# A three-stage attention block: first key products ahead of the queries, feature sums on GpSimd, and a new order around them

## The chip, the core and the metric

The kernel runs on one core of a Trainium2 chip. A core has a matrix engine (TensorE, in profiles PE, with its weight loads as PEld), a vector engine (DVE), a scalar engine (ACT), GpSimd (POOL) and a queue engine (SP) that here only starts transfers. PE writes to PSUM, eight banks of 2 KB per partition; DVE and ACT read PSUM, POOL doesn't. The metric is the device time of one execution in microseconds, lower is better.

## The reference

One token array x (512 x 512, float32) goes through three residual layers.

```python
x = x + _L0_xattn_ref(_layernorm(x), ctx, ctx, ...)   # 16 heads of 32, 8192 context rows, softmax
x = x + _L0_attn_ref(_layernorm(x), ...)              # linear attention
x = x + _L0_ffn_ref(_layernorm(x), ...)               # 512 -> 2048 -> 512, quantized, gelu
...
q_proj = _elu1(jnp.einsum('bhnd,hdf->bhnf', q, proj_matrix))   # 128 features for each head
k_proj = _elu1(jnp.einsum('bhnd,hdf->bhnf', k, proj_matrix))
kv = jnp.einsum('bhnf,bhnd->bhfd', k_proj, v)
attn = jnp.einsum('bhnf,bhfd->bhnd', q_proj, kv)
k_sum = k_proj.sum(axis=2)
z = 1.0 / (jnp.einsum('bhnf,bhf->bhn', q_proj, k_sum) + 1e-08)
```

The quantized layer needs the smallest and largest value of its whole input before it can scale it, and of its whole hidden layer before the second product.

## The kernel before, in words

P = 128 partitions; the 512 tokens are four tiles t (NT), the 512 columns four groups c or g (NE) of four heads each (HG). The context is read in 16 blocks of 512 rows. Every PE, DVE, ACT and POOL instruction wrapped in `in_order` stays in the order in which the program text issues it on its engine; each engine then waits only for data and free buffers.

**Opening.** `load_w` (L130), `load_cols` and `load_ctx` (L309) put the transfers on SP's queue: x, Wq, bq, Wk, context block 0, bk, Wv, block 1 and the small rows. DVE normalizes x (`norm_factors`, L150 on: mean and variance, square root on ACT, reciprocal, one correction step). PE transposes it (L349), DVE and ACT copy the result to `xnT`, PE projects the queries (L136) and ACT adds their bias.

**Blockwise products.** Keys and values of a block are made by `blockwise` (L456): a 2 x 2 block scheme with seven products n = 1 to 7, where four need sums of weights (`sums_of_weights`, L373) and of the context (`sums_of_ctx`, L391), both made by POOL. Products 1 and 2 take plain blocks. A product is four steps of four matmuls each (`by_columns`, L403); `evict` then copies or adds its PSUM tile into the four quadrants C11 to C22 of kT or vt, on ACT for the first, on DVE (L493, L496) for the others. Tiles come from `ps_m`, which has two banks. The order is 1, 6, 7, 5, 4, 2, 3.

**Maxima.** Before the loop, `common_maxima` (L583) finds one bound per group g from the scores of 128 keys (L598): two reductions on DVE for each group (L603), then a reduction over groups, a transposition (L614), a second reduction, a diagonal, and a product with ones that spreads it over the partitions (L621). Products of the first values block stand between these: `spread` puts four steps behind each of four groups, `ahead(4)` twice takes four from the queue.

**The loop.** 256 units (block, group, key tile): scores by PE (L757, 64-wide halves), exp by ACT (L766), sums of the weights by DVE (L775), weighted values by PE one unit later (L702). Between scores and weighted values PE takes steps of the next block's products from a queue, as many as `due` says, so that a block is ready when its units start. The last block has its own branch.

**Hand-over.** Output sums of the four token tiles (L867, PSUM tiles `po4`), addition to x and statistics (`added`), normalization in halves of two tiles (`normed`), transposition in halves (`turned_tokens`, L890), then the second attention's values (`values`, L903).

**Linear attention.** For each group g: keys and queries (`projected`, L971), features (`key_features` L1014, `query_features` L1025: PE into the four banks of `ps_f`, ACT exp and relu L993, DVE min and sum L997), `products` (L1038: values times features, and ones times features for the sum over tokens), `turned`, `attended` (L1061), `divided` (a reciprocal L1071). The calls are written out by hand from L1082 on, so that PE makes the next group's keys or queries while ACT and DVE make features. Then the output sums (`out_sums`) and `out_added` with the running extremes.

**Quantized layer.** `norm_factors`, `extremes` (a transposition L1159, a product with ones L1166), rounding and clipping (L1189 to L1194), first product with gelu, extremes again, second product. `keep_busy(n)` issues n bf16 matmuls whose result nobody reads.

A second copy of the program, with exact maxima, follows in an `If` and isn't executed here.

Of the kernel before, what the change touches and what calls it, by code (L numbers as in the profile page):

```python
# [26 lines left out]
def network(  # L27
# [125 lines left out]
    def norm_factors(name, st):  # L153

        n = st.shape[1]

        def op(what, do, *args):
            d = small.tile([P, n], F32, name=f"{name}_{what}", bufs=1)
            in_order(do(d, *args))
            return d  # L160

        mv = small.tile([P, n, 2], F32, name=f"{name}_mv", bufs=1)
        for t in range(n):
            in_order(nc.vector.bn_aggr(mv[:, t, :], st[:, t, :]))
        ve = op("ve", nc.vector.tensor_scalar, mv[:, :, 1], LN_EPS, None, ALU.add)
        sd = op("sd", nc.scalar.activation, ve, AF.Sqrt)
        r0 = op("r0", nc.vector.reciprocal, sd)

        e0 = op("e0", nc.vector.tensor_tensor, r0, r0, ALU.mult)
        e1 = op("e1", nc.vector.tensor_tensor, e0, ve, ALU.mult)  # L170
        e2 = op("e2", nc.vector.tensor_scalar, e1, -0.5, 1.5, ALU.mult, ALU.add)
        rstd = op("rstd", nc.vector.tensor_tensor, r0, e2, ALU.mult)
        return mv[:, :, 0], rstd
# [104 lines left out]
    with ExitStack() as actx:  # L278
# [25 lines left out]

        def load_ctx(b):
            if b >= total:
                return
            ct[b] = ap2.tile([P, NE, KB], F32, name="ct")
            nc.sync.dma_start(  # L309
                ct[b], ctxT[:, ts(b % NB, KB)].rearrange("(c p) k -> p c k", p=P)  # L310
            )
# [4 lines left out]
        wq_sb, wv_sb, wk_sb = place_w(), place_w(), place_w()  # L316
        load_w(Wq, wq_sb)
        bq_sb = load_cols(bq, NE, "bq_sb")
        load_w(Wk, wk_sb)
        load_ctx(0)  # L320
        bk_sb = load_cols(bk, NE, "bk_sb")
# [23 lines left out]
        with tc.tile_pool(name="ps_q", bufs=NE, space=PSUM) as ps_q:  # L345
            pts = [ps_q.tile([P, S], F32, name="pxt") for _ in range(NE)]
            for t in range(NT):
                for c in range(NE):
                    in_order(nc.tensor.transpose(  # L349
                        pts[c][:, ts(t, P)], xn[:, t, ts(c, P)], ident  # L350
                    ))
            for c in range(NE):
                if c % 2 == 0:
                    nc.vector.tensor_copy(xnT[:, c, :], pts[c])
                else:
                    nc.scalar.copy(xnT[:, c, :], pts[c])
        for g in range(NE):
            pq = ps_m.tile([P, S], F32, name="pq", tag="pt")
            project(pq, lambda c: wq_sb[:, c, ts(g, P)], lambda c: xnT[:, c, :])
            nc.scalar.activation(  # L360
                qT[:, g, :], pq, AF.Identity, bias=bq_sb[:, g : g + 1]
            )
# [29 lines left out]

        if not exact:
            of_keys = sums_of_weights(wk_sb)
            sums_of_ctx(0)
            of_values = sums_of_weights(wv_sb)
        for t in range(NT):
            in_order(nc.gpsimd.tensor_add(xs[:, t, :], xs[:, t, :], bo_bc))
# [57 lines left out]
        def blockwise(b, keys):  # L456
# [44 lines left out]
            def evict(n):  # L501
# [3 lines left out]
                if n == 1:  # L505
                    in_order(nc.scalar.copy(C11, ps))
                elif n == 6:
                    add(C12, C11, ps)
# [10 lines left out]
                elif n == 2:  # L519
                    add(C11, C11, ps, 0)  # L520
                elif n == 3:
                    add(C12, C12, ps)
# [10 lines left out]
            for n in (1, 6, 7, 5, 4, 2, 3):  # L533
# [12 lines left out]
            return steps  # L546

# [35 lines left out]
        def common_maxima(mp, ps_x):  # L583
# [22 lines left out]


            steps = blockwise(0, False)
            spread([(g,) for g in range(NE)], scores, steps[: 4 * NE])
            queue[:0] = [(1, step) for step in steps[4 * NE :]]  # L610
            ahead(4)
            in_order(nc.vector.tensor_reduce(top, tops, AX.X, ALU.max))
            pt = ps_x.tile([P, 2, S], F32, name="pm", tag="scm")
            in_order(nc.tensor.transpose(pt[:NE, 0, :P], top, ident))  # L614
            ahead(4)
# [3 lines left out]
            ))  # L619
            pb = ps_x.tile([P, 2, S], F32, name="pb", tag="scm")  # L620
# [59 lines left out]
        with ExitStack() as mctx:  # L680
            mp = mctx.enter_context(tc.tile_pool(name="mp", bufs=1, side="right"))
            ps_x = mctx.enter_context(tc.tile_pool(name="ps_x", bufs=3, space=PSUM))
            for step in keys_of(0) if exact else blockwise(0, True):
                step()
# [215 lines left out]
        def values(t, copy):  # L900
            ps = ps_m.tile([P, E], F32, name="pv2", tag="pt")
            for c in range(NE):
                in_order(nc.tensor.matmul(  # L903
# [14 lines left out]
        for t in range(2, 4):  # L918
            output_sums(po4[t], t, range(NE), Z, wo_sb)
            added(t, po4[t], x_st[1], t - 2)  # L920
        turned_tokens(0)
        normed(1)
        warm_up(AF.Exp)
        values(0, nc.scalar.copy)
        turned_tokens(1)
        values(1, nc.scalar.copy)
# [24 lines left out]
    with ExitStack() as lctx:  # L951
# [14 lines left out]
        kT2, qT2, kf, qf, kvT, kvl = {}, {}, {}, {}, {}, {}  # L966
# [41 lines left out]
        def key_features(g, between):  # L1008

            ps = ps_f.tile([P, HG, S], F32, name="feat")  # L1010
            for t in range(NT):
                for j in range(HG):
                    rows = ts(j, D)
                    in_order(nc.tensor.matmul(  # L1014
                        ps[:, j, ts(t, F)], lhsT=kT2[g][rows, ts(t, P)],
                        rhs=proj_sb[rows, g, :], start=True, stop=True,
                    ))
            kf[g] = elu1(ps, by_head, between)

        def query_features(g, between):  # L1020

            ps = ps_f.tile([P, HG, S], F32, name="feat")
            for j in range(HG):
                rows = ts(j, D)
                in_order(nc.tensor.matmul(  # L1025
                    ps[:, j, :], lhsT=proj_sb[rows, g, :], rhs=qT2[g][rows, :],
                    start=True, stop=True,
                ))
            qf[g] = elu1(ps, by_token, between)

        def products(g):
# [3 lines left out]
            for i in range(2):  # L1035
                for t in range(NT):
                    for j in range(HG):
                        in_order(nc.tensor.matmul(  # L1038
                            ps[ts(j, D), i, :],
                            lhsT=ones_c if i else va[:, t, ds(g * P + j * D, D)],  # L1040
                            rhs=kf[g][:, j, ts(t, F)],
                            start=(t == 0), stop=(t == NT - 1),
                        ))
# [57 lines left out]
        products(3)  # L1101
        att = attended(2, every, (ps_a, "av"))
# [4 lines left out]


        po = [ps_m.tile([P, E], F32, name="po", tag="pt") for _ in range(2)]
# [3 lines left out]

        def out_sums(t, groups):
            output_sums(po[t], t, groups, aT, wout_sb)

        def out_added(t):
# [7 lines left out]
            smallest(x_lo[:, one], xs[:, t, :])  # L1125

        out_sums(0, [0, 1]), out_sums(1, [0, 1])
# [3 lines left out]
        out_sums(2, [0, 1])  # L1131
# [5 lines left out]
        out_sums(3, [0, 1]), out_sums(2, [2, 3]), out_sums(3, [2, 3])  # L1137
# [57 lines left out]


    mean, rstd = norm_factors("y", y_st)
# [17 lines left out]
    mm = extremes("q1", y_ext, (lambda: norm(0), lambda: (norm(1), norm(2))))  # L1215
# [57 lines left out]
    def keep_busy(n):  # L1273


        for _ in range(n):
            in_order(nc.tensor.matmul(
                pys[NT - 1], lhsT=w2_q[:, 0, :P], rhs=w2_q[:, 0, :], start=True, stop=True
            ))

    keep_busy(8)
# [3 lines left out]
    mm = extremes("q2", h_ext, (lambda: keep_busy(1), lambda: keep_busy(6)))  # L1285
# [105 lines left out]
```

## Time and profile before

| | us |
|---|---|
| median of 3 runs (1124.95 to 1125.51) | 1125.46 |
| the profiled execution | 1124.31 |
| its span | 1122.4 |
| opening and queries, to the first key product | 26.9 |
| key products of block 0 | 12.4 |
| maxima | 18.4 |
| the loop to the first output sum | 903.8 |
| hand-over, to the second attention's keys | 24.6 |
| linear attention to the last output sum | 78 |
| quantized layer | 58 |

PE is busy for 1080.2 of the 1122.4 us, DVE for 927.7, ACT for 633.5, POOL for 163.4. A group of the profile is a source line on an engine; `a<-b,c` names the tile written and those read. A float32 matmul of the program shows as two hardware matmuls. The idle time in brackets is that of the engine just before the row, with what ended it.

### The profile page before, as it was taken

How to read it: one execution, taken by the hardware profiler on the slowest of the kernel's cores; microseconds unless marked ns; L12 is line 12 of the kernel's file. 1: busy time of each engine (PE TensorE's matmuls, PEld its weight loads, DVE VectorE, ACT ScalarE, POOL GpSimd, SP SyncE). 2: the span in 40 equal slices, each digit the busy share in tenths (PEclk: the TensorE clock that was granted, in tenths of full speed). 3: DMA queues.
4: the chain of work that ended last, by engine and by line, in shares of the span. 5: the costliest groups of instructions: out<-in, count | busy, mean ns of one | idle time of the engine just before them, and what ended most of it. 6: DMA issues, size and time to landing. Idle time of an engine off the chain costs nothing.

```text
span 1122.4 us, 30765 instructions
## 1 busy us (share of the span) xinstructions
PE 1080.2 (96%) x14207; PEld 407.2 (36%) x14210; DVE 927.7 (83%) x863; ACT 633.5 (56%) x425; POOL 163.4 (15%) x82
## 2 busy tenths in 40 slices
PE   6999999999999999999999999999999999999876
PEld 3433333333333333333333333333332322344332
DVE  3678999998888888888888888888887878656896
ACT  2055555556666666666665555555555566336353
POOL 3430303003303030303030303030300000000000
PEclk9999999999999999999999999999999999999988
DMA  7021222120212030212010101010110021130001
GB/s 262 3 95 58 77 58 96 39 76 30 80 46 68 31 95 30 67 58 67 31 58 2 39 2 40 2 39 2 40 39 2 2 76 39 38 151 1 1 1 40
DMA packets 24744, 55.54 MB, mean 49 GB/s; under 512 B 1952, under 2 KB 2464, under 8 KB 24352
## 3 DMA queue, kind: packets, MB, share of 16 engines
q1 hardware_dynamic: 24320, 52.97, 14.3%
q8 instruction: 113, 1.85, 0.6%
q10 hardware_dynamic: 288, 0.52, 0.1%
q14 instruction: 23, 0.19, 0.1%
HBM read 48.25 MB, written 5.24 MB: 48 GB/s over the span
## 4 chain that ended last, share of the span: by engine, by line
PE 89%; DVE 4%; ACT 4%; issue 1%; DMA 0%; ACTq 0%; DVEq 0%
PE pm L403 36%; PE sc L757 24%; PE av L702 18%; ACT ex L766 4%; PE po L867 2%; PE pq L971 2%; PE pv L903 1%; PE pq L136 1%; DVE unchanged L143 1%; PE pys L1292 1%; DVE de L1071 1%; PE att L1061 1%; PE dn L720 0%; DVE f L997 0%; PE feat L1014 0%
## 5 line engine op out<-in xcount | busy, mean ns | idle before, releaser
L766 ACT ACTIVATE ex<-sc,bias 128x2048 f32<-128x2048 f32 x256 | 504.0, 1969 | 360.8 <-PE sc L757 359.0
L775 DVE TENSOR_TENSOR acc<-acc,ex 128x2048 f32<-128x2048 f32 x248 | 581.6, 2345 | 73.5 <-ACT ex L766 72.8
L757 PE MATMUL sc<-qT,kT 32*64 32x512 f32 x4096 | 285.2, 613 | 6.9 <-ACT ex L766 6.7
L702 PE MATMUL av<-ex,vt 128*32 128x512 f32 x2048 | 266.9, 593 | 0.0
L757 PEld LDWEIGHTS sc<-qT,kT 32*64 32x64 f32 x4096 | 59.7, 129 | 221.8 <-ACT ex L766 199.7
L391 POOL TENSOR_TENSOR tt<-ct 128x512 f32<-128x512 f32 x32 | 55.6, 1738 | 577.7 <-DMA ct<-in_ctxT 399.7
L403 PE MATMUL pm<-w,tt 128*32 128x256 f32 x2048 | 126.8, 382 | 0.0
L403 PE MATMUL pm<-tt,w 128*32 128x256 f32 x1920 | 118.0, 382 | 0.0
L493 DVE TENSOR_TENSOR vt<-vt,pm 128x512 f32<-128x512 f32 x112 | 75.4, 685 | 31.3 <-PE pm L403 30.1
L403 PE MATMUL pm<-w,ct 128*32 128x256 f32 x1536 | 98.7, 383 | 0.0
L391 POOL TENSOR_TENSOR tt<-ct,tt 128x512 f32<-128x512 f32 x32 | 93.3, 2915 | 1.3
L403 PE MATMUL pm<-ct,w 128*32 128x256 f32 x1440 | 92.3, 383 | 0.0
L403 PEld LDWEIGHTS pm<-w,tt 128*32 128x32 f32 x2048 | 59.8, 109 | 86.0 <-issue 53.4
L702 PEld LDWEIGHTS av<-ex,vt 128*32 128x32 f32 x2048 | 65.4, 110 | 55.4 <-issue 14.0
L403 PEld LDWEIGHTS pm<-tt,w 128*32 128x32 f32 x1920 | 56.7, 109 | 77.0 <-issue 45.4
L403 PEld LDWEIGHTS pm<-w,ct 128*32 128x32 f32 x1536 | 43.5, 109 | 72.5 <-issue 48.6
L403 PEld LDWEIGHTS pm<-ct,w 128*32 128x32 f32 x1440 | 41.1, 109 | 67.9 <-issue 44.5
L493 DVE TENSOR_TENSOR kT<-kT,pm 128x512 f32<-128x512 f32 x60 | 40.9, 681 | 27.4 <-PE pm L403 26.4
L496 DVE SCALAR_TENSOR_TENSOR kT<-pm,bk_sb,kT 128x256 f32<-128x256 f32 x90 | 39.1, 474 | 4.5 <-PE pm L403 4.5
L714 DVE TENSOR_TENSOR Z<-Z,av 128x512 f32<-128x512 f32 x60 | 40.7, 678 | 0.0
L993 ACT ACTIVATE er<-feat 128x1024 f32<-128x1024 f32 x32 | 30.2, 1030 | 8.9 <-PE feat L1014 6.7
L997 DVE SCALAR_TENSOR_TENSOR f<-er 128x1024 f32<-128x1024 f32 x16 | 19.4, 1219 | 15.1 <-ACT er L993 15.1
(176 smaller groups left out, 558.0 us busy)
## 6 DMA issues: line engine op xcount, KB each, us to landing
ct<-in_ctxT SPq DMA_DIRECT2D x16, 1024.0 KB, 5.3
wraw<-in_W1T SPq DMA_DIRECT2D x16, 512.0 KB, 3.8
wraw<-in_W2T SPq DMA_DIRECT2D x16, 512.0 KB, 3.7
wd<-wquant SPq DMA_DIRECT2D x16, 256.0 KB, 2.4
w_q<-wd SPq DMA_DIRECT2D x2, 2048.0 KB, 10.5
w<-in_w_qkv SPq DMA_DIRECT2D x3, 1024.0 KB, 5.1
w<-in_Wq SPq DMA_DIRECT2D x1, 1024.0 KB, 7.4
w<-in_Wk SPq DMA_DIRECT2D x1, 1024.0 KB, 9.6
```

The lines of the kernel that those rows point to most:

```text
L391: in_order(nc.gpsimd.tensor_tensor(tt[b][:, i], x, y, ALU.subtract))
L403: in_order(nc.tensor.matmul(ps[ts(j, D)], lhsT=lhsT[:, ts(j, D)], rhs=rhs, start=start, stop=stop))
L493: in_order(nc.vector.tensor_tensor(dst, src, ps, ALU.add))
L496: in_order(nc.vector.scalar_tensor_tensor(dst[:, m, :], ps[:, m, :], bk_sb[:, 2 * i + m : 2 * i + m + 1], src[:, m, :], ALU.add, ALU.add,))
L702: in_order(nc.tensor.matmul(av[g][ts(j, D), :], lhsT=vt[b][:, k, ds(g * P + j * D, D)], rhs=ex[:, j, :], start=(k == 0), stop=(k == NC - 1),))
L714: in_order(nc.vector.tensor_tensor(Z[:, g, :], Z[:, g, :], ps, ALU.add))
L757: in_order(nc.tensor.matmul(sc[ts(h, P // 2), j, :], lhsT=kT[b][rows, g, ds(k * P + h * P // 2, P // 2)], rhs=qT[rows, g, :], start=not ex ...
L766: in_order(nc.scalar.activation(ex, sc, AF.Exp, bias=bias[:, g : g + 1], scale=SCALE))
L775: in_order(nc.vector.tensor_tensor(acc[:, g], acc[:, g], ex, ALU.add))
L867: in_order(nc.tensor.matmul(po, lhsT=lhsT[:, c, ts(t, P)], rhs=w[:, c, :], start=(c == 0), stop=(c == NE - 1),))
L971: in_order(nc.tensor.matmul(ps, lhsT=wt[:, c, ts(g, P)], rhs=ynT[:, c, :], start=(c == 0), stop=(c == NE - 1),))
L993: in_order(nc.scalar.activation(er[-1][:, d].rearrange("p a n -> p (a n)"), ps[h], function))
```

## The change

The transfers of the opening come in another order and Wk and block 0 in halves. Ten products of the identity with itself and the first key product are issued ahead of PE's transpositions, the second key product between the transpositions and the queries. The order of the seven products becomes 1, 2, 6, 7, 5, 4, 3, with C12 as the place of the first.

```diff
+        ct[0] = ap2.tile([P, NE, KB], F32, name="ct")
+        for h in range(2):
+            half = ts(h, NE // 2)
             nc.sync.dma_start(
-                ct[b], ctxT[:, ts(b % NB, KB)].rearrange("(c p) k -> p c k", p=P)
+                wk_sb[:, half, :], Wk.rearrange("(c p) n -> p c n", p=P)[:, half, :]
             )
...
+            nc.sync.dma_start(ct[0][:, half, :], ctx_of(0)[:, half, :])
+        bk_sb = load_cols(bk, NE, "bk_sb")
         load_w(Wq, wq_sb)
         bq_sb = load_cols(bq, NE, "bq_sb")
-        load_w(Wk, wk_sb)
-        load_ctx(0)
-        bk_sb = load_cols(bk, NE, "bk_sb")
         load_w(Wv, wv_sb)
...
-                    in_order(nc.scalar.copy(C11, ps))
+                    in_order(nc.scalar.copy(C12, ps))
                 elif n == 6:
-                    add(C12, C11, ps)
+                    add(C12, C12, ps)
...
-                    add(C11, C11, ps, 0)
+                    add(C11, C12, ps, 0)
...
-            for n in (1, 6, 7, 5, 4, 2, 3):
+            for n in (1, 2, 6, 7, 5, 4, 3):
...
+        def first_keys(n):
+
+            for step in key_steps[: 4 * n]:
+                step()
+            del key_steps[: 4 * n]
...
+            for _ in range(10):
+                in_order(nc.tensor.matmul(
+                    pts[0][:, :P], lhsT=ident, rhs=ident, start=True, stop=True
+                ))
+            first_keys(1)
+            for t in range(NT):
...
+        first_keys(1)
+        for g in range(NE):
+            pq = ps_m.tile([P, S], F32, name="pq", tag="pt")
```

In the norm factors the correction step has one instruction less on its chain, and a caller may put an instruction beside the square root. In the maxima the fourth group's scores follow at once, and six steps and one step stand in other places than four and four.

```diff
+        vh = op("vh", nc.vector.tensor_scalar, ve, -0.5, None, ALU.mult)
+        meanwhile()
         r0 = op("r0", nc.vector.reciprocal, sd)
...
         e0 = op("e0", nc.vector.tensor_tensor, r0, r0, ALU.mult)
-        e1 = op("e1", nc.vector.tensor_tensor, e0, ve, ALU.mult)
-        e2 = op("e2", nc.vector.tensor_scalar, e1, -0.5, 1.5, ALU.mult, ALU.add)
-        rstd = op("rstd", nc.vector.tensor_tensor, r0, e2, ALU.mult)
+        e1 = op("e1", nc.vector.tensor_tensor, e0, vh, ALU.mult)
+        rstd = op("rstd", nc.vector.scalar_tensor_tensor, e1, 1.5, r0, ALU.add, ALU.mult)
...
-            spread([(g,) for g in range(NE)], scores, steps[: 4 * NE])
-            queue[:0] = [(1, step) for step in steps[4 * NE :]]
-            ahead(4)
+            last = 4 * (NE - 1)
+            spread([(g,) for g in range(NE - 1)], scores, steps[:last])
+            queue[:0] = [(1, step) for step in steps[last:]]
+            scores(NE - 1)
             in_order(nc.vector.tensor_reduce(top, tops, AX.X, ALU.max))
+            ahead(6)
             pt = ps_x.tile([P, 2, S], F32, name="pm", tag="scm")
             in_order(nc.tensor.transpose(pt[:NE, 0, :P], top, ident))
-            ahead(4)
...
+            ahead(1)
             pb = ps_x.tile([P, 2, S], F32, name="pb", tag="scm")
```

At the hand-over the first half's transpositions come in the middle of token tile 3's output sums, the second half's in the middle of values(1), which takes its tile from `ps_a`.

```diff
-        for t in range(2, 4):
-            output_sums(po4[t], t, range(NE), Z, wo_sb)
-            added(t, po4[t], x_st[1], t - 2)
...
+        output_sums(po4[2], 2, range(NE), Z, wo_sb)
+        output_sums(po4[3], 3, range(2), Z, wo_sb)
         turned_tokens(0)
+        added(2, po4[2], x_st[1], 0)
+        output_sums(po4[3], 3, range(2, NE), Z, wo_sb)
+        added(3, po4[3], x_st[1], 1)
         normed(1)
         warm_up(AF.Exp)
         values(0, nc.scalar.copy)
-        turned_tokens(1)
-        values(1, nc.scalar.copy)
+        values(1, nc.scalar.copy, ps_a, "av", lambda: turned_tokens(1))
```

In the linear attention the features are made in 64-wide halves, POOL adds the four token tiles of a group's key features, and `products` multiplies that sum by ones once instead of each tile. The output sums of token tiles 0 to 3 stand in other places.

```diff
+                    for h in range(2):
+                        in_order(nc.tensor.matmul(
+                            ps[ts(h, P // 2), j, ts(t, F)],
+                            lhsT=kT2[g][rows, ds(t * P + h * P // 2, P // 2)],
+                            rhs=proj_sb[rows, g, :], start=True, stop=True,
+                        ))
             kf[g] = elu1(ps, by_head, between)
+
+            half = lp.tile([P, HG, 2 * F], F32, name="kf_half", bufs=1)
+            kf_sum[g] = lp.tile([P, HG, F], F32, name="kf_sum")
+            in_order(nc.gpsimd.tensor_tensor(
+                half, kf[g][:, :, : 2 * F], kf[g][:, :, 2 * F :], ALU.add
+            ))
+            in_order(nc.gpsimd.tensor_tensor(
+                kf_sum[g], half[:, :, :F], half[:, :, F:], ALU.add
+            ))
...
+                    ps[ts(j, D), 1, :], lhsT=ones_c, rhs=kf_sum[g][:, j, :],
                     start=True, stop=True,
...
+        po = [ps_m.tile([P, E], F32, name="po", tag="pt")]
...
+        out_sums(0, [0, 1])
         att = attended(2, every, (ps_a, "av"))
...
-        out_sums(0, [0, 1]), out_sums(1, [0, 1])
+        out_sums(1, [0, 1]), out_sums(2, [0, 1])
         halves = [ts(i, S // 2) for i in range(2)]
         att = attended(3, halves[0], (ps_a, "av"))
         divided(3, halves[0], att)
-        out_sums(2, [0, 1])
+        out_sums(3, [0])
...
-        out_sums(3, [0, 1]), out_sums(2, [2, 3]), out_sums(3, [2, 3])
+        out_sums(3, [1]), out_sums(2, [2, 3]), out_sums(3, [2, 3])
```

In the quantized layer the minimum of the last token tile is taken beside the square root, and there are more idle matmuls: 16 and 2 ahead of the first product, 32 instead of 8 ahead of the second extremes.

```diff
+    nothing = ps_m.tile([P, E], F32, name="nothing", tag="pt")
+    keep_busy(nothing, 16)
+    last = NT - 1
+    mean, rstd = norm_factors(
+        "y", y_st, lambda: smallest(x_lo[:, last:NT], xs[:, last, :])
+    )
...
+        (lambda: (norm(0), keep_busy(nothing, 2)), lambda: (norm(1), norm(2))),
...
-    keep_busy(8)
+    idle = pys[NT - 1]
+    keep_busy(idle, 32)
```

## The prediction

> **What bounds the kernel now.** I read the span by stretches first, cut where the program changes its work; columns are length, then busy time of PE, weight loads, DVE, ACT and POOL, then the granted clock.
>
> ```profile
> core 0: us, PE busy (x) PEld busy (x) DVE busy (x) ACT busy (x) POOL busy (x), PEclk, DMA share, GB/s
> 0.00:12.96 12.96, 4.20 (x18) 3.77 (x18) 8.42 (x39) 3.50 (x6) 0.82 (x5) 1.00 0.85 295
> 12.96:26.96 14.00, 14.00 (x36) 6.07 (x40) 0.55 (x1) 2.61 (x5) 9.29 (x8) 1.00 0.72 253
> ...
> 39.29:57.70 18.41, 16.05 (x231) 7.34 (x227) 14.47 (x19) 0.58 (x1) 2.88 (x3) 1.00 0.01 2
> ...
> 360.00:860.00 500.00, 499.73 (x7312) 182.66 (x7312) 431.92 (x328) 308.33 (x179) 77.22 (x32) 1.00 0.11 36
> ...
> 961.50:986.20 24.70, 23.19 (x69) 11.01 (x66) 19.05 (x36) 3.88 (x9) 0.00 (x0) 1.00 0.12 42
> 986.20:1043.60 57.40, 55.45 (x527) 27.66 (x525) 33.99 (x36) 31.55 (x39) 0.38 (x1) 1.00 0.19 74
> 1043.60:1069.00 25.40, 19.76 (x90) 7.60 (x90) 20.64 (x46) 8.58 (x12) 0.00 (x0) 0.97 0.00 1
> ```
>
> The long loop is PE without a gap, and its products are only reordered. So I price the edges: PE work that goes, and PE work that moves into gaps. Next I read the timeline at those edges (start, length, operation, idle time before it and its releaser).
>
> ```profile
> 9.14 3.62 PE L349 MATMUL pxt<-ident,xn 128*128 128x128 f32 x16 [6.19 <-DVE xn L341]
> ...
> 12.33 5.06 POOL L373 TENSOR_TENSOR w<-w 128x512 f32<-128x512 f32 x4 [11.90 <-DMA w<-in_Wk]
> ...
> 12.96 14.00 PE L136 MATMUL pq<-xnT,w 128*128 128x512 f32 x32 [0.20 <-DVE xnT L354]
> ...
> 53.71 0.27 PE L614 MATMUL pm<-ident,top 128*4 128x128 f32 x1 [0.88 <-DVE top L612]
> ...
> 57.09 0.38 PE L621 MATMUL pb<-diag,ones_g 4*128 4x4 f32 x2 [1.25 <-DVE diag L617]
> ...
> 977.68 3.67 PE L903 MATMUL pv<-w,ynT 128*128 128x512 f32 x8 [1.27 <-ACT ynT L898]
> ...
> 1013.31 1.08 PE L1038 MATMUL kv<-f,va 128*32 128x128 f32 x32 [0.46 <-ACT kvl L1052]
> ...
> 1014.20 1.06 PE L1038 MATMUL kv<-f,ones_c 128*32 128x128 f32 x32
> ```
>
> A program matmul in f32 is two hardware ones. The gaps: PE idle until 9.14, 2.1 us in the maxima, 1.27 at the hand-over; and the ones products cost PE as much as the value products. Last, POOL, which now gets work that PE waits for:
>
> ```profile
> 37.05 1.29 POOL L391 TENSOR_TENSOR tt<-ct 128x512 f32<-128x512 f32 x1
> ...
> 70.94 3.43 POOL L391 TENSOR_TENSOR tt<-ct 128x512 f32<-128x512 f32 x1
> ...
> 251.80 1.56 POOL L391 TENSOR_TENSOR tt<-ct 128x512 f32<-128x512 f32 x1 [7.14 <-PE pm L403]
> ```
>
> **1 Opening, -0.9 (bounds -1.5 and +0.8).** By issue and landing, Wq lands at 1.64 + 7.4 = 9.04, Wk at 2.66 + 9.6 = 12.26, Wv at 5.37 + 12.3 = 17.67, so a megabyte takes 2.7 to 3.2. In the new order the halves of Wk and block 0 land near 7.4, 9.0, 10.6 and 12.3, and Wq third, near 15.0. PE: ten products of the identity with itself from 3.5 to some 7.8 (20 hardware matmuls at 0.21, half clock), then product 1 from 9.0. At full clock it takes 1.76 (12.33/7 in the timeline), at half clock 3.5. The transposes, ready at 9.14, now queue behind it: 10.8 to 12.8 or 12.5 to 14.4 (16 at 0.12 to 0.13 as in the pyn row, 1.04 for 8, instead of 3.1). Product 2 follows while DVE and ACT copy xnT: to 14.6 or 16.2; queries from 15.0 (waiting for Wq) or 16.2, 14.0 long; five products more, 8.8: 37.8 or 39.0 against 39.29 now. The warm-up should leave the clock between these; I take 38.4. Half landings 1 us later give +0.8. At no cost: the norm factors lose one step of 0.2, hidden behind product 1; POOL's sums of Wk start at 10.6 rather than 12.33; those of Wv still wait for the queries and are done about 35, ten before their first product.
>
> **2 Maxima, -1.9 (-2.6 to -1.0).** From the first scores (S = 39.29) the first weights come at 57.73, S+18.4. The new order puts one product after each of three groups, the fourth group's reductions ahead of other evictions. DVE then binds: four reductions of 2.36 plus two evictions of 0.68 from S+1.2 end at S+12.1 with the maximum. PE has done its scores, three products and six steps by S+12.6; transpose, reduction, diagonal, one step, broadcast, copy (0.3+0.4+0.2+0.1+0.4+0.3 by the rows) bring the weights to S+14.4. That is 4.0 earlier, but five steps fewer are done (9 left in the queue, not 4); each is eight matmuls, 0.43, and the loop has no PE gap to hide them: +2.1.
>
> **3 The loop, 0 (-0.3 to +1.0).** Products 1 and 2 need no POOL sums, the same number of evictions stands on DVE and ACT, product 3 of the order still waits for the buffer of the first. DVE is 94% busy between 120 and 240; that is the cover that would fail.
>
> **4 Hand-over to the second attention, -1.45 (-1.7 to -0.8).** PE: four output groups end at 968.4 (eight of 0.86), token tile 2 at 971.8, half of tile 3 at 973.55, when yn (973.39) is there; transposes to 974.9, rest of tile 3 to 976.6, values(0) without its 1.27 wait to 980.05, half of values(1) to 981.8, transposes to 982.95, rest to 984.65. The first keys start there instead of 986.11. DVE's added(2) now stands behind a copy that waits for PE; the chain added(2), added(3), normed(1) ends at 980.65, before 981.8. DVE's two reductions of acc move to 983 to 987.6; the key copy after them comes 0.2 late, and 3.4 of values(2) hide that.
>
> **5 Linear attention, -1.6 (-2.6 to +1.0).** Ones products: 32 hardware matmuls become 8; 32 take about 0.88 net, so 0.66 goes, four times; three lie on PE's path, the fourth before a wait for f (1.27 idle at 1043.62). Features as 64-wide halves: twice the instructions, the same array time, since eight tiles of L757 start within 0.05 us; the first load is 128 ns against 181, so 0.05 less each, 0.3 over six. New: PE waits for POOL's sums. 1536 elements at 1.27 per 512 are 3.85, and each f of DVE (1.22, two SBUF inputs) that falls inside stops POOL as the acc additions do at 70.94. Time from f to the first ones product now: 7.1, 6.2, 5.6 and 5.6. Group 1 loses 0.66 of it because products(0) shrinks, and two f operations fall in: 1007.9 + 3.85 + 2.4 = 1014.2 against 1013.5: late by 0.7. Others are in time. 3 x 0.66 + 0.3 - 0.7 = 1.6.
>
> POOL also changes its program after the all-reduce at 987. The row at 251.80 shows what that takes: the all-reduce ended at 244.66 (244.29 + 0.37), the operands had by the blocks' 57 us rhythm been there since about 236, and 7.14 passed. The page GPSIMD Engine Reference (Instruction dispatch) of the Trainium skill says that the first call after new code is loaded pays some 6 us with no instruction to show for it; the trace agrees with 7.14, though its releaser column names PE. Here it runs to about 996, and f of group 0 comes at 998 (999.7 less part 4), so it is hidden by 2 us.
>
> **6 Output sums and last additions, -0.25 (-0.9 to +0.6).** One tile's sums fill the 1.27. But tile 2 now sits in banks that the last features hold until ACT has read them (1047.05 + 3.77 = 1050.8), so its two sums run 50.9 to 52.65 ahead of the attention that started at 51.60; a shorter sum between the halves makes that up, and DVE reaches out_added(0) 0.3 late. Tile 2 is then done before DVE asks (0.34 wait gone), and the moved minimum fills the square root's wait (0.24 of it).
>
> **7 Clock, -0.5 (-1.2 to +0.3).**
>
> ```profile
> 1063.88:1067.29 3.41, 0.48 (x2) 0.00 (x0) 3.18 (x13) 0.13 (x1) 0.00 (x0) 1.00 0.01 2
> 1067.29:1070.70 3.41, 1.02 (x4) 0.71 (x5) 3.03 (x16) 1.56 (x3) 0.00 (x0) 0.50 0.00 0
> ```
>
> After a stretch with PE 0.48 of 3.41 busy the grant halves, and again at 1094.6. The fillers: 16 of 0.213 (8 took 1.89 with their tail at 1088.72) from about 63.4 to 66.8, free by the 1069.06 transposition; 32 from 1088.7 to 1095.5, before 1097.1. The small products on the way cost 0.37 and 0.58 at half clock, 0.27 and 0.38 in the maxima at full: 0.3 twice, mostly. If the second filler ran at half clock it would end at 1102.4, +5; 0.213 says it doesn't. TensorE: Matmul & The Clock Gate (the clock gate, Part 1) of the Trainium skill gives a free-running window of 3.4 us; the two rows agree.
>
> **Sum.** -0.9 -1.9 +0 -1.45 -1.6 -0.25 -0.5 = -6.6. The profiled execution took 1124.31 (span 1122.4 and 1.9 around it), so 1117.7; the runs' median is 1125.46, 1.15 more, so 1118.9 by that measure, which I predict.
>
> **Rivals.** (a) The opening is bound by landings and the clock terms give nothing: without 1 and 7, and with group 1 and 2 sums late by 1 more each, 1118.9 + 1.4 + 2 = 1122.3. For it: Wq third in a full queue; DMA is 85% busy there. Against: PE idles 8 us at the start. 0.2. (b) The sums by POOL become the wait, slower: if POOL gets its 3.43 per 512 throughout, a sum takes 10.2 against 5.5 to 7.1, late 3.1, 4.7, 4.6, 4.6, 17 in all: 1136. It decides from about 7.2 per sum, where lateness eats the 6.6. Against: f takes 1.22 twice in 6.8 us, acc 2.3 of 3.55. GPSIMD Engine Reference (Key points) names two SBUF inputs on DVE as the contention; 1.29 against 3.43 agrees. 0.06. (c) The work doesn't go but reappears: the loop is DVE's, evictions of five more steps wait, 3 gives +2 and 5 only breaks even: 1122.5 to 1125, no change that can be told. 0.07. (d) Everything at its better bound: 1114.5 to 1116. 0.07.
>
> **Chances.** Forecast 0.6 (own range 1116.4 to 1121.4). 0.2% is 2.25 us, what a measurement here can tell: faster below 1123.2. Faster 0.87 (forecast, d and nearly all of a), same 0.07, slower 0.06. Range 1115.3 to 1122.8.
>
> **What would show it.** First scores near 38.4; first weights 14.4 after them; the second attention's first keys 23.1 after the first output sum, not 24.6 (961.53 to 986.11); ones products of group 1 alone with a wait on POOL, under 1 us; out_added(0) no earlier against the last features than now; grant 1.00 at the two small transpositions. Wrong if PE waits for POOL in three groups, if scores come after 39.3, or if PE shows idle time between 120 and 860.

## The result, and the profile after

The changed kernel takes 1119.17 us, the median of 8 runs (1117.25 to 1121.99), against 1125.16 (1124.15 to 1125.51) for the kernel before beside it: ratio 0.9952, 95% interval 0.9943 to 0.9961. It is faster by 6.0. The profiled execution has a span of 1116.9 against 1122.4, 5.5 less.

Each stretch below runs from one landmark's start on PE to the next, read from the timelines of the two kernels; the prediction's column adds up its terms.

| stretch | before | changed | predicted | measured |
|---|---|---|---|---|
| start to first scores | 39.29 | 37.39 | -0.9 | -1.90 |
| to first weights | 18.44 | 14.31 | -4.0 | -4.13 |
| loop, to first output sum | 903.80 | 905.92 | +2.1 | +2.12 |
| hand-over, to the second attention's first keys | 24.58 | 22.46 | -1.45 | -2.12 |
| linear attention, output sums, additions, to the first small transposition | 82.95 | 83.84 | -1.85 | +0.89 |
| to the second products | 32.21 | 31.72 | -0.5 | -0.49 |
| to the end | 21.13 | 21.26 | 0 | +0.13 |

So the sum (-5.5 for -6.6) hides two errors of opposite sign: the opening, the maxima and the hand-over gave 1.8 more than was said, and the second attention, where 1.85 was to go, lost 0.9. The windows of the changed kernel, with the columns and most of the stretches shown of before (the same times; from the hand-over on the changed kernel is 4 to 6 us ahead):

```profile
0.00:12.96 12.96, 8.86 (x78) 7.59 (x82) 8.21 (x38) 3.98 (x6) 2.83 (x7) 1.00 0.86 309
...
39.29:57.70 18.41, 17.63 (x263) 7.54 (x255) 14.41 (x19) 4.08 (x3) 4.35 (x4) 1.00 0.19 59
360.00:860.00 500.00, 499.73 (x7300) 182.23 (x7296) 432.90 (x325) 308.47 (x179) 78.16 (x32) 1.00 0.11 36
961.50:986.20 24.70, 24.70 (x71) 11.84 (x70) 18.54 (x42) 4.12 (x8) 0.38 (x1) 1.00 0.21 65
986.20:1043.60 57.40, 54.01 (x611) 24.25 (x609) 35.22 (x31) 34.66 (x43) 15.51 (x8) 1.00 0.16 65
1043.60:1069.00 25.40, 22.73 (x92) 10.52 (x94) 21.14 (x59) 6.04 (x10) 0.00 (x0) 0.87 0.00 1
```

PE is busy twice as long in the first 12.96 (8.86 for 4.20), has no gap at the hand-over (24.70 for 23.19), and the loop is as full as it was. (The granted clock is on record only from its first rise, 7.13 here and 12.57 before; the 1.00 of the first row says nothing of the time ahead of that.) The last row is the odd one: its granted clock is 0.87, where it was 0.97. Two stretches at half clock lie in it, from 1065.26 to 1068.68 in the quantized layer, where the kernel before had one too, and from 1044.78 to 1048.20, which is new. The timeline of PE in the changed kernel, at the end of the linear attention, shows where the new one comes from:

```profile
1034.01 0.40 PE L1091 MATMUL kv<-kf_sum,ones_c 128*32 128x128 f32 x8
1035.23 1.98 PE L898 MATMUL po<-w,aT 128*128 128x512 f32 x4 [0.82 <-DVE qT L1012]
1037.15 1.92 PE L1112 MATMUL att<-f,kvl 128*32 128x512 f32 x16
...
1039.37 1.11 PE L1073 MATMUL feat<-qT,proj_sb 32*64 32x512 f32 x16
1040.41 1.98 PE L898 MATMUL po<-w,aT 128*128 128x512 f32 x4
1044.42 3.46 PE L898 MATMUL po<-w,aT 128*128 128x512 f32 x4 [2.02 <-ACT er L1029]
1047.80 1.24 PE L1112 MATMUL att<-f,kvl 128*32 128x256 f32 x16
```

Tile 2's sums wait 2.02 for ACT to read the last features' banks, as the prediction said they would; but then the same four matmuls that took 1.98 take 3.46. Windows of the same kernel, cut where the granted clock changes (column after the five busy times):

```profile
1037.95:1041.37 3.42, 3.42 (x32) 1.05 (x25) 1.89 (x2) 1.46 (x2) 0.00 (x0) 1.00 0.00 0
1041.37:1044.78 3.41, 1.39 (x4) 0.49 (x3) 3.38 (x3) 3.00 (x4) 0.00 (x0) 1.00 0.00 0
1044.78:1048.20 3.42, 3.42 (x8) 0.88 (x10) 1.43 (x2) 0.00 (x0) 0.00 (x0) 0.50 0.00 0
```

A stretch of 3.41 with PE busy for 1.39 of it is followed by one at half clock, with PE full. TensorE: Matmul & The Clock Gate (HAM oscillation — how this bites in real kernels) of the Trainium skill puts its rule as no PE gap over some 3.4 us; here a gap of 2.02 is enough, so the measurement decides. (It is not always enough: e2_ones_by_pe below.)

### The profile page after: what moved, and what is told of

It is laid out like the page before. It is cut to its first block, busy times and chain, and to the rows that moved or that the text cites. A ratio compares the mean times of both kernels' runs of the same rounds, so it can differ in the third digit from the quotient of the medians.

```text
span 1116.9 us, 31051 instructions
## 1 busy us (share of the span) xinstructions
PE 1089.1 (98%) x14331; PEld 409.7 (37%) x14336; DVE 932.2 (83%) x863; ACT 633.7 (57%) x425; POOL 177.8 (16%) x90
## 3 DMA queue, kind: packets, MB, share of 16 engines
q1 hardware_dynamic: 24352, 52.97, 14.3%
## 4 chain that ended last, share of the span: by engine, by line
PE 88%; ACT 5%; DVE 5%; issue 1%; DMA 1%; SPq 0%; DVEq 0%; ACTq 0%
PE pm L388 35%; PE sc L788 24%; PE av L733 18%; ACT ex L797 4%; PE po L898 2%; PE pq L1007 2%; PE pq L136 1%; DVE unchanged L143 1%; PE pv L936 1%; PE pys L1356 1%; DVE de L1122 1%; ACT er L1029 1%; PE att L1112 1%; DMA ct<-in_ctxT 1%; DVE tops L631 0%
## 5 line engine op out<-in xcount | busy, mean ns | idle before, releaser
L383 POOL TENSOR_TENSOR tt<-ct 128x512 f32<-128x512 f32 x32 | 62.4, 1950 | 573.4 <-DMA ct<-in_ctxT 519.8
L383 POOL TENSOR_TENSOR tt<-ct,tt 128x512 f32<-128x512 f32 x32 | 85.3, 2666 | 1.3
```

The costliest lines, as they stand in the source:

```text
L383: in_order(nc.gpsimd.tensor_tensor(tt[b][:, i], x, y, ALU.subtract))
```

## The experiments

Spans are of the profiled execution. The kernel before had medians of 1124.84 to 1125.34 beside these runs.

**The order of the output sums (e1_sums_order).** The old order, all else as changed:

```diff
-        out_sums(0, [0, 1])
         att = attended(2, every, (ps_a, "av"))
...
-        out_sums(1, [0, 1]), out_sums(2, [0, 1])
+        out_sums(0, [0, 1]), out_sums(1, [0, 1])
...
-        out_sums(3, [0])
+        out_sums(2, [0, 1])
```

> The changed kernel with the output sums in the old order: tiles 0 and 1 after the last features, tile 2 between the halves of attended(3). Theory (the two sums of tile 2 wait 2.02 for ACT's reading of the last features' banks, the clock halves after that gap, and the attention behind them starts 2.7 late): the wait of the output sums on ACT goes, no granted clock of 0.5 between 1040 and 1050, attended(3) first half starts about 1044.3 instead of 1047.80, span 1114.4 instead of 1116.9, and the kernel is faster than the changed one. Rival 1 (DVE's reciprocals and additions set the end there, PE's gap costs nothing): span within 0.6 of 1116.9. Rival 2 (the early sums of tile 0 are worth what the wait costs): attended(2) waits 1.3 again, span 1116.3 or more.

Measured: 1116.6 (1116.12 to 1117.83, 5 runs), ratio to before 0.9928 (0.9914 to 0.9941); span 1114.7. PE's timeline in this run:

```profile
1034.07 0.40 PE L1091 MATMUL kv<-kf_sum,ones_c 128*32 128x128 f32 x8
1036.42 1.92 PE L1112 MATMUL att<-f,kvl 128*32 128x512 f32 x16 [1.95 <-DVE f L1033]
...
1039.69 3.70 PE L898 MATMUL po<-w,aT 128*128 128x512 f32 x8
1044.39 1.07 PE L1112 MATMUL att<-f,kvl 128*32 128x256 f32 x16 [1.01 <-DVE f L1033]
```

The attention starts at 1044.39, as the theory said, and first keys to first small transposition take 81.41 for 83.84. So the new order of the sums costs 2.43 here, and this version is faster than both kernels. Attended(2) waits 1.95, but it also starts 0.73 earlier than behind tile 0's sums.

**Is it the clock? (e11_filled_wait).** Back to the changed kernel, with PE kept busy in the gap:

```diff
+        for _ in range(2):
+            in_order(nc.tensor.matmul(
+                po[1], lhsT=aT[:, 0, ts(1, P)], rhs=wout_sb[:, 0, :],
+                start=True, stop=True,
+            ))
         out_sums(1, [0, 1]), out_sums(2, [0, 1])
```

> The changed kernel with two products of no use (four of 0.44) ahead of tile 1's output sums, so that PE is busy for all but 0.3 of the 2.02 in which the sums of tile 2 wait for ACT. Theory (that gap halves the clock of what follows, which costs 1.5 beside the wait itself): no granted clock of 0.5 near 1045, tile 2's first two sums in 2.0 instead of 3.45, attended(3) first half at 1046.4 instead of 1047.80, span 1115.4. Rival 1 (the halving has another cause): 3.45 stays, span 1116.9. Rival 2 (PE's place there does not count, DVE sets the end): attended(3) earlier by 1.4, span within 0.4 of 1116.9.

The timeline of this run:

```profile
1040.65 1.98 PE L1183 MATMUL po<-w,aT 128*128 128x512 f32 x4
1042.47 1.88 PE L898 MATMUL po<-w,aT 128*128 128x512 f32 x4
1044.65 1.98 PE L898 MATMUL po<-w,aT 128*128 128x512 f32 x4 [0.30 <-ACT er L1029]
1046.56 1.07 PE L1112 MATMUL att<-f,kvl 128*32 128x256 f32 x16
```

Useless work makes the sums 1.48 shorter; first keys to first small transposition: 82.19. So of the 2.43, 1.65 is the half clock and 0.78 the order itself (82.19 less 81.41). The span, 1116.1, fell by only 0.8, for this execution began 0.23 later and took 0.6 longer from the second products to the end; the median, 1119.14 (1117.94 to 1119.35, 4 runs), is that of the changed kernel. So the 1.65 is shown for the profiled execution, which is the fastest of the four, and not for the median. The mean granted clock, in which the time ahead of the first rise counts as full, was 0.994 to 0.996 in the eight runs of the changed kernel and 0.998 to 0.999 in these four: every one of them has less half clock behind the rise, and what the other three lost instead is not known.

**What POOL's additions are worth (e2_ones_by_pe, e12_ones_old_sums).** The same edit twice, on the changed kernel and on e1_sums_order:

```diff
-            in_order(nc.gpsimd.tensor_tensor(
-                half, kf[g][:, :, : 2 * F], kf[g][:, :, 2 * F :], ALU.add
-            ))
...
+                        ps[ts(j, D), 1, :], lhsT=ones_c,
+                        rhs=kf[g][:, j, ts(t, F)],
+                        start=(t == 0), stop=(t == NT - 1),
```

> The changed kernel with the sums over tokens taken back from POOL: 32 ones products for each group on PE, no POOL additions. Theory (two of the four savings of 0.66 reach the end, groups 0 and 1; that of group 2 falls into a wait of 0.91 before the next key features, that of group 3 into one of 0.82 before the output sums): last features 1.3 later against the second attention's first keys (59.29 now), span 1118.2. Rival 1 (all of groups 0 to 2 count): 2.0 later, span 1118.9. Rival 2 (the last features hang on ACT and DVE alone, the products are hidden): 59.3, span 1116.9.

> e1_sums_order with the ones products back on PE (32 a group, no POOL additions): the same edit as e2_ones_by_pe, where the order of the output sums does not open the long gap. Theory (two of four savings reach the end, and nothing takes them back here): first keys to last features 59.7 instead of 58.51, all behind the same, span 1115.9, median 1117.8 against 1116.6. Rival 1 (what POOL's additions save is given back here too): from the first keys to the first small transposition 81.4 as in e1_sums_order, span 1114.7. Rival 2 (three savings count): 60.5, span 1116.7.

In both, last features come 1.3 later after the first keys (60.61 for 59.29, 59.82 for 58.51), the theory's two savings of 0.66. In e12 that stays: 82.67 for 81.41 to the small transposition, 1118.45 (1117.95 to 1119.59) for 1116.6. In e2 it seems not to: 83.45 for 83.84. But there the clock was not halved, though PE is as busy before the gap, and the gap is again 2.02. It lies across the end of one of the clock's stretches (the last section shows their grid), so that PE is busy for 1.72 of the stretch with the larger part of it, and not for 1.39 (windows of e2):

```profile
1044.38:1047.79 3.41, 1.72 (x4) 0.41 (x3) 3.38 (x3) 3.41 (x4) 0.00 (x0) 1.00 0.00 0
1047.79:1051.20 3.41, 3.08 (x21) 1.26 (x22) 2.12 (x2) 0.30 (x2) 0.00 (x0) 1.00 0.00 0
```

Where the gap lies in the grid is chance. Set against e11, which isn't halved either (82.19), e2 is 1.26 later: POOL's additions gain the same in the changed kernel. (e2's median is 1120.45, 1120.01 to 1120.77; its span, 1119.0, also holds an opening 2.4 later, below.)

**How far POOL can be late (e5_pool_twice)**, on e1_sums_order, the first addition issued twice:

```diff
+            in_order(nc.gpsimd.tensor_tensor(
+                half, kf[g][:, :, : 2 * F], kf[g][:, :, 2 * F :], ALU.add
+            ))
```

> e1_sums_order with POOL's first addition of each group issued twice (same data), so 2.4 more for each sum. Theory (the sums are done 2.4, 0.8, 1.9 and 1.9 before PE asks for them, groups 0 to 3; behind group 2 a wait of 0.9 and behind group 3 one of 1.95 take up what is late): PE waits for POOL in group 1 by 1.7 to 2.8 and by about 0.5 in groups 2 and 3, span 1116.4 to 1117.6 instead of 1114.7. Rival 1 (there is more slack than the end times show): no wait on POOL over 0.5, span 1115.0 or less. Rival 2 (POOL's contention with DVE makes the sums much longer, as the prediction's second rival has it): waits in all four groups, span over 1119.

1127.42 (1125.01 to 1129.16, 10 runs), ratio to before 1.0023 (1.0014 to 1.0033): slower than before. PE's timeline at group 1:

```profile
1007.42 1.08 PE L1088 MATMUL kv<-f,va 128*32 128x128 f32 x32 [0.46 <-ACT kvl L1106]
1010.90 0.43 PE L1094 MATMUL kv<-kf_sum,ones_c 128*32 128x128 f32 x8 [2.40 <-POOL kf_sum L1066]
1011.26 1.25 PE L1051 MATMUL feat<-proj_sb,kT 32*64 32x128 f32 x64
1012.44 5.31 PE L1007 MATMUL pq<-ynT,w 128*128 128x512 f32 x8
```

The theory had the wait right and what follows wrong. The wait halves the clock (eight matmuls 5.31 for 3.70), attended(2) later meets another half-clock stretch (3.31 for 1.92), and the waits behind groups 2 and 3 absorb nothing, since the work that they wait for has moved as well. First keys to last features: 66.77 for 58.51, 8.3, of which 3.0 is half clock. The sums took 6.1 to 8.0 here (mean 6.8) and cost more than the whole change gained: the limit of some 7.2 in the prediction's second rival was a little too generous. The signs of rival 2 came (PE waits for POOL by 0.21, 2.40, 0.44 and 0.46, span 1123.6), its reason only in part: in groups 0 and 1 the sums are 0.9 longer than the second addition explains, in groups 2 and 3 they are not.

**The opening (e3_no_warm_up, e10_old_opening).** The first takes the ten warm-up products out of the changed kernel; the second gives e1_sums_order the old opening:

```diff
-        ct[0] = ap2.tile([P, NE, KB], F32, name="ct")
-        for h in range(2):
...
+        load_w(Wk, wk_sb)
+        load_ctx(0)
...
-            first_keys(1)
```

> The changed kernel without the ten warm-up products. Theory (they bring the granted clock up before product 1): clock 0.5 until about 12.3, product 1 takes 3.5 instead of 1.93, first scores at 39.0 instead of 37.39, span 1118.5. Rival (product 1 and the transposes run at their pace anyway, or the queries wait for Wq, which lands at 14.3): first scores by 37.8, span within 0.5 of 1116.9.

> e1_sums_order with the old opening: Wq, Wk and block 0 loaded whole in that order, no warm-up, transposes and queries first, then the seven key products. Theory (the opening's gain is what PE did not do before 9 us, and nothing behind depends on it): first scores 39.3 instead of 37.45, all stretches behind the same, span 1116.6. Rival 1 (POOL's sums of Wk and of block 0 come too late for the seven products in one row): first scores 40 or later. Rival 2 (most of the gain is given back later): span 1115.3 or less.

e3: clock up at 13.05 only, first scores at 39.52, span 1119.0, median 1120.85 (1120.35 to 1122.12); 1.82 of the 2.13 is the half clock, 0.31 a later landing: the theory's mechanism, 0.5 beyond its 39.0. e10: first scores at 39.31, all stretches behind within 0.2 of e1_sums_order, span 1116.4, median 1118.38 for 1116.6. Its four runs lie within 0.41, the five of e1_sums_order within 1.71, the changed kernel's eight within 4.74. The opening's gain is real, and not the same in every execution. PE's timeline in the changed kernel:

```profile
3.52 4.21 PE L550 MATMUL pxt<-ident 128*128 128x128 f32 x20 [0.57 <-DVE ident L98]
8.89 1.93 PE L388 MATMUL pm<-ct,w 128*32 128x256 f32 x32 [1.16 <-DMA ct<-in_ctxT]
10.76 1.97 PE L556 MATMUL pxt<-ident,xn 128*128 128x128 f32 x16
12.65 1.93 PE L388 MATMUL pm<-ct,w 128*32 128x256 f32 x32
14.52 14.00 PE L136 MATMUL pq<-xnT,w 128*128 128x512 f32 x32
```

and in e2_ones_by_pe, whose opening is the same code:

```profile
3.53 4.01 PE L550 MATMUL pxt<-ident 128*128 128x128 f32 x20 [0.57 <-DVE ident L98]
9.65 3.21 PE L388 MATMUL pm<-ct,w 128*32 128x256 f32 x32 [2.11 <-DMA ct<-in_ctxT]
```

There block 0's first half landed 0.75 later, the gap after the warm-up was 2.11 for 1.16, and the clock fell from 10.14 to 13.55: first scores at 39.77.

**A longer warm-up and filled gaps (e8_long_warm_up, e9_gaps_filled).** On e1_sums_order, 16 products for 10; and, in e9, single sums moved into the gaps as well and 37 fillers for 32:

```diff
-            for _ in range(10):
+            for _ in range(16):
...
+        out_sums(0, [0])
         att = attended(2, every, (ps_a, "av"))
...
-        out_sums(0, [0, 1]), out_sums(1, [0, 1])
+        out_sums(0, [1]), out_sums(1, [0, 1]), out_sums(2, [0])
```

> e1_sums_order with 16 instead of 10 warm-up products. Theory (the changed kernel's runs spread over 4.7 because the first halves land between 8.8 and 9.7, and in the late ones PE's gap after the warm-up halves the clock once more, as in the run with the old ones products, where the first scores came at 39.77): no granted clock of 0.5 behind 7.2 in the opening, first scores between 37.4 and 38.2, median 1116.0 or less against 1116.6, runs within 1.5. Rival (the longer warm-up only delays product 1): first scores 0.3 or more later than 37.45 with the same landings, median 1117 or more.

> e1_sums_order with its gaps filled: 16 warm-up products, one sum of tile 0 ahead of attended(2) (its bank comes free 1.2 before the attention may start), one of tile 2 ahead of attended(3) and one of tile 3 between its halves, 37 fillers before the second transposition. Theory (the runs differ by where a gap of 1 to 2 us meets the clock's windows; filled gaps keep the grant, and DVE's last wait of 0.34 goes): no granted clock of 0.5 between 7.2 and 1110, attended(2) and attended(3) at most 0.15 later than in e1_sums_order, span 1114.0 to 1114.5 against 1114.7, median 1116.0 or less against 1116.6, runs within 1.5. Rival (the sums moved ahead delay the attention and everything behind): span 1115 or more.

Neither gains: 1117.30 (1116.48 to 1117.85) and 1117.14 (1116.83 to 1118.70) against 1116.6. In e8 the opening kept its clock (scores at 37.49), but the gap of 1.95 before attended(2) met a stretch that halved it from 1037.70, 0.8 lost. In e9 the grant came only at 8.80, so the 16 products ran to 9.79 and held product 1 up some 0.6 beyond the 0.13 that it starts behind its data elsewhere; and tile 2's early sum put attended(3) 0.35 later. That was made up for: first keys to first small transposition take 81.33 for 81.41, so all that e9 lost it lost in the opening. The median of 1116.0 or less came in neither, and the rivals' numbers came without their reasons: in e8 product 1 was not delayed, and in e9 the early sums cost nothing at the end. The ranges overlap with that of e1_sums_order, so neither is shown to be slower.

**Hand-over, maxima, fillers (e4_old_hand_over, e6_old_maxima, e7_few_fillers).** The first on the changed kernel, the others on e1_sums_order (parts of the three edits, in this order):

```diff
-        values(1, nc.scalar.copy, ps_a, "av", lambda: turned_tokens(1))
+        turned_tokens(1)
+        values(1, nc.scalar.copy)
...
-            scores(NE - 1)
...
-            ahead(6)
...
-    keep_busy(nothing, 16)
...
-    keep_busy(idle, 32)
+    keep_busy(idle, 8)
```

> The changed kernel with the old order at the hand-over (tiles 2 and 3, both transpositions and the values one after the other). Theory (what the new order gains there stays): first output sum to the second attention's first keys 24.6 instead of 22.46, span 1119.0. Rival (part of it is given back, since the second attention's first features wait for DVE or ACT work that has moved behind): the keys 24.6, but first keys to last features shorter than 59.3 by 1 or more, span 1118 or less.

> e1_sums_order with the old order of the maxima (a product after each of four groups, four steps before the maximum and four after the transposition). Theory (4.1 gained before the first weights, 2.1 given back in the loop, whose PE has no gap): first scores to first weights 18.4 instead of 14.3, first weights to first output sum 903.8 instead of 905.9, span 1116.7. Rival 1 (the five steps cost the loop nothing): 905.9 stays, span 1118.8. Rival 2 (the loop is DVE's and gives back everything): span 1114.7.

> e1_sums_order without the 16 and 2 filler products of the first quantization and with 8 instead of 32 ahead of the second. Theory (the fillers only spare the small products on the way the half clock): from the first small transposition to the first product 5.3 instead of 5.14, from the second to the second products 4.1 instead of 3.9, span 1115.0 to 1115.2. Rival 1 (nothing, since the granted clock falls there with the fillers too): 1114.7. Rival 2 (the large products behind start at half clock and lose up to 1.7 each time): span over 1116.5.

e4: hand-over 24.57 for 22.46, first keys to last features 59.30; 1120.85 (1120.08 to 1121.32). Nothing of its 2.11 is given back. e6: first weights 19.04 after the scores, loop 903.77 for 905.91; span 1117.2, median 1119.98 (1119.07 to 1121.42). So 4.7 less 2.1; the loop does take the five steps back, and only these. (The first weights come 0.6 later than in the kernel before because the fifth product, the last ahead of the maximum, is now product 5, with two additions on DVE, and not product 4, with one: PE waits 1.48 for the maximum instead of 0.88.) e7: 1117.79 (1117.44 to 1118.01); from the first small transposition to the second products 33.31 for 31.93. The fillers are worth 1.4, between theory and second rival. Its timeline has what the theory left out:

```profile
1064.27 3.04 PE L1289 MATMUL pyt<-ident,yf 128*128 128x128 f32 x13 [0.23 <-DVE yf L1273]
1067.10 4.85 PE L1312 MATMUL ph<-yqT,w_q 128*128 128x512 bf16 x16
```

The first 16 large products take 4.85 for 3.87, because the clock stays at half until 1069.58. In the kernel before it had come back at 1074.12, 0.2 ahead of its first product (1074.32).

## Why the prediction was right, and where it was not

**1 Opening, -0.9 said, -1.90 measured.** The chain was right step by step; the size was off, mainly because 38.4 was taken between its two clock cases, 37.8 and 39.0. The profiled execution is the full-clock one (1.93 for product 1 against 1.76 said), with the queries at 14.52 where this case had 15.0, as Wq landed at 14.3. e2 is the half-clock one, at 39.77, with its halves landing later. A mean of two cases is no case. Rival (a), no gain from the opening, falls with e10.

**2 and 3 Maxima and loop, -1.9 said, -2.01.** First weights 14.31 after the first scores (14.4 said), five steps given back at 2.12 (2.1 said); e6 shows both, with 4.7 and 2.1. PE's idle time in the loop's middle, 0.27 of 500, did not change, so rival (c) falls.

**4 Hand-over, -1.45 said, -2.12, beyond its bound of -1.7.** The two blocks of eight transposes were put at 1.35 and 1.15, though the row of before shows 1.04. In the changed kernel the next group starts 0.88 after each:

```profile
969.74 1.04 PE L921 MATMUL pyn<-ident,yn 128*128 128x128 f32 x8
970.62 1.88 PE L898 MATMUL po<-w,Z 128*128 128x512 f32 x4
...
977.48 1.04 PE L921 MATMUL pyn<-ident,yn 128*128 128x128 f32 x8
978.36 1.88 PE L936 MATMUL pv<-w,ynT 128*128 128x512 f32 x4
```

(PE's timeline, changed kernel.) Two times 0.88 for 1.35 and 1.15 is 0.74 less; the other pieces together took 0.07 more than was put.

**5 Linear attention, -1.6 said, -1.26.** By e12 against e1. Three savings of 0.66 less 0.7 of waiting were expected, and 0.3 from the features. It was two savings with no wait: behind group 2 PE waits 0.91 before the key features of group 3 (0.23 before the change), so that saving goes nowhere. POOL's sum is 3.7, and 4.7 in group 1, where it meets DVE's f; the forecast of 3.85 + 2.4 there was too long, and it is done 0.8 before PE asks. PE waits for POOL in no group, so rival (b) falls. The features in halves gain nothing: with 32 ones products a group, e12 takes 59.82 from the first keys to the last features, the kernel before 59.73. The POOL rows of the changed kernel:

```profile
995.35 2.35 POOL L1060 TENSOR_TENSOR kf_half<-f 128x1024 f32<-128x1024 f32 x1 [11.63 <-PE pv L936]
997.77 1.28 POOL L1063 TENSOR_TENSOR kf_sum<-kf_half 128x512 f32<-128x512 f32 x1
1002.08 2.36 POOL L1060 TENSOR_TENSOR kf_half<-f 128x1024 f32<-128x1024 f32 x1 [3.03 <-DVE f L1033]
1004.52 2.25 POOL L1063 TENSOR_TENSOR kf_sum<-kf_half 128x512 f32<-128x512 f32 x1
```

POOL's first addition starts at 995.35, 1.6 after its f (where group 1 needs 0.14) and 11.6 after the end of POOL's all-reduce, 983.71. So what the prediction calls the change of program was not over before f, as it said; by the other runs with these additions POOL starts 10.5 to 11.9 after the all-reduce wherever f is there earlier, and 12.5 after it, 0.2 behind f, in e4_old_hand_over, where f comes later. That is more than the 7.14 of before; no row shows what POOL does in that time. PE doesn't feel it, since the sum is there 1.85 before it is needed.

**6 Output sums and last additions, -0.25 said, +2.15: the step that failed.** The prediction has "its two sums run 50.9 to 52.65 ahead of the attention that started at 51.60" and "a shorter sum between the halves makes that up". The wait was found, and its length (the banks come free 5.05 after the last features begin, 4.96 by the prediction's 1050.8 against 1045.84). Missing were two things. "One tile's sums fill the 1.27" put 1.98 of work, which may start 0.82 into that gap, ahead of attended(2): everything behind came 0.78 later, ACT's reading too. And what the gap does to the clock was priced for the small products of part 7, but not here: 1.65. The shorter stretch between the halves (2.23 for 2.91) does not make up for that: DVE starts out_added(0) 14.64 after the last features begin, where it was 12.56, so 2.1 late and not 0.3. The wait of 0.34 in front of tile 2's addition did go. The other half of the term, the minimum moved beside the square root, held: 82.67 in e12 against 82.95 before the change, 0.28 for 0.24 said.

**7 Clock, -0.5 said, -0.49.** Both small transpositions take 0.27 at full clock. Of the gain 0.12 lies ahead of the first products and 0.40 ahead of the second, where 0.3 twice was said. That the fillers are worth 1.4 with the new times of the work behind (e7), and 0.5 against the kernel before, is chance of where the stretches of half clock lie.

The total is near because parts 1 and 4 (1.7 better) offset most of part 6 (2.4 worse): that the measured 1119.17 lies 0.3 from the forecast 1118.9 is luck, while the direction and most terms are not. Whether the wide scatter of the changed kernel's runs comes from the opening and the gap at 1042 is argued from e2, e10 and e11 and not shown run by run. Half clock alone doesn't order them: the slowest, 1121.99, has a mean granted clock of 0.995, as the profiled execution (1118.67).

## What to carry to other kernels

A wait in front of PE costs its own length and then, if it leaves PE idle for most of one of the clock's stretches of 3.4, half the speed of what comes next: price both, or put work, even useless work, into the gap. When a saving on one engine lies ahead of a wait for another, it pays only up to that wait; follow it to the next landmark before counting it once per group. And where data land at a varying time, look at each case by itself and not at the mean of them.

## What the runs showed of the hardware

**The clock falls on a fixed grid and for gaps of 2 us.** In all 14 profiles the changes of the granted clock within one execution lie on a grid of 3.413 us (the distances between them are whole multiples of it to within a thousandth), whose place differs from execution to execution: the clock first rose at 6.45 to 8.81 in those with a warm-up from 3.52. This agrees with the free-running window that TensorE: Matmul & The Clock Gate (Part 1) of the Trainium skill describes. Every trace was cut on its grid, from the first rise to the last product, and PE's busy time added up in each stretch at full clock. Of 10 stretches with PE busy for up to 0.42 of them, all were followed by half clock; of 38 with 0.43 to 0.63, 14 were; of 59 with 0.64 to 0.80, none. So in these runs 2 us of idle time within one stretch always cost the clock, 1.2 us or less never did, and between them it went either way; what decides there is not shown. The same code pays or not as the grid falls: the gap of 1.95 ahead of attended(2) cost nothing more in e1_sums_order and 0.8 in e8_long_warm_up.

**POOL beside DVE.** An addition of 512 elements took 1.28 alone and 2.25 where one f of DVE (two SBUF inputs, 1.23) fell almost wholly inside, and 0.15 of a second: POOL was held up for 0.97, most of the f's own length. It goes the other way round too: an f that started with 0.5 or more of an addition of POOL still to run took 1.68 in the changed kernel (at 998.45) and 1.61 to 2.34 in e5_pool_twice. In the kernel before, e2_ones_by_pe and e12_ones_old_sums, where POOL adds nothing beside it, no f takes more than 1.26.
